# The ternary feed-forward of the last layer, taken from a stage of its own into the chain of attention units

## The chip, the cores and the metric

The kernel runs on one core of one Trainium2 chip. The metric is the device time of one execution in microseconds; lower is better. The profile names the engines of the core PE (matrix multiply), PEld (its weight loads), DVE (vector), ACT (scalar), POOL (GpSimd) and SP (which issues most transfers).

## The reference

A decoder of four layers works on an activation `x` of 4 batches × 256 tokens × 128 features, which is 8 tiles of 128 tokens, two to a batch. Each layer adds a self-attention, a cross-attention and a feed-forward to `x`. This case is about the last layer, whose feed-forward has ternary weights and activations rounded to 8 bits:

```python
x = x + _L3_attn_ref(_layernorm(x), ...)            # 16 heads of 8, low-rank, causal
x = x + _L3_xattn_ref(_layernorm(x), ctx_1024, ...) # 16 heads of 8, 512 keys
x = x + _L3_ffn_ref(_layernorm(x), L3_ffn_w1, L3_ffn_w2)

def _quant_act(x):                                  # per token
    scale = 127.0 / jnp.clip(jnp.max(jnp.abs(x), axis=-1, keepdims=True), EPS, None)
    xq = jnp.clip(jnp.round(x * scale), -128.0, 127.0) / scale
    return x + jax.lax.stop_gradient(xq - x)
def _bitlinear(x, w):
    return jnp.einsum('bsi,oi->bso', _quant_act(x), _quant_weight(w))
h = jax.nn.gelu(_bitlinear(x, w1), approximate=False)   # 128 -> 512
return _bitlinear(h, w2)                                # 512 -> 128
```

## The kernel before, in words

All of `x` stays on chip (`x[t]` is tile t). The stages follow one another: `layer_0`, `ffn0`, `layer_1`, `ffn1`, the linear and the latent attention of layer 2, `ffn2`, `layer_3`, `quantised_ffn`, and eight transfers that write `x` to `out`. Instructions are written in an order that the code sets, and each engine works through its own in that order.

`layer_3` builds eight `Unit`s: units 0 to 3 are the self-attentions of the four batches, units 4 to 7 their cross-attentions. `woven` runs them as one chain. It cuts each unit into steps, gives each step a time on a scale on which one unit takes 1.0, sorts by that time and emits. What falls behind a unit's own 1.0 is carried into the next unit. So in a stretch of the chain these stand side by side:

- the scores of the next unit by rows of queries (`rows_of`): PE writes `s`, and DVE reads it for the row's largest value `mx` (L477 to L481; with a mask, L481 goes over 128×512 values and a short read of the accumulator follows). In layer 3 two row tiles and two column tiles make a beat;
- the scores of this unit by columns of keys (`columns_of`): PE adds the mask (L522), less the maximum (L529) and the score (L535) into `s`, and ACT takes the exponential into `pr` (L552);
- the weighted sum of values (`weighted`, L571) into the only bank `o`, which ACT copies out at its end (`os`, L577); then division (L589, L591), transposing and `added` (L606 on PE, L610 on DVE), which adds the batch's result to `x`;
- the prelude of the unit after the next (`norm`, `source`, `queries`, `keys`), and `values`.

All tiles of `s` come from seven banks (`BANKS`: `"s1": 7`). A list `u.after` holds steps that are to follow a unit's `added`; the code spreads them over 2.6 units of time:

```python
late += spread(u.after, at + 2.1 * lag, at + 2.1 * lag + 2.6)
```

In this kernel only `layer_1` fills it (its strided cross-attention).

`quantised_ffn` comes after the chain has ended, has its own pools, and goes tile by tile: norm, `quantise` (largest absolute value `am`, L1950; scale `qs`, L1951 to L1954; its inverse `un`, L1956 and L1957; rounding and clipping `q`, L1959 and L1960), transposing through PE (`pt`, L311) with DVE as the reader (`qT`, L1964), the hidden matmul (`sc`, L1973), the exact Gelu on ACT (`h`, L1975), the same `quantise` on 512 values, four transposes, four matmuls (`ms`, L1979), and the sum into `x` (L1983). Only the Gelu needs another function table on ACT than the exponential of the chain. The ternary weights were made ready much earlier (`ternary_weights`).

Of the kernel before, what the change touches and what calls it, by code (L numbers as in the profile page):

```python
# [22 lines left out]
F32 = mybir.dt.float32  # L23
BF16 = mybir.dt.bfloat16
# [3 lines left out]
AF = mybir.ActivationFunctionType  # L28
ALU = mybir.AluOpType
AX = mybir.AxisListType  # L30
PSUM = bass.MemoryType.PSUM

P = 128
B, S, D, H = 4, 256, 128, 16
NT = B * S // P
# [5 lines left out]
EPS = 1e-5  # L41
# [3 lines left out]
MAGIC = 12582912.0  # L45
# [138 lines left out]
def decoder(ctx: ExitStack, tc: tile.TileContext, dr, out):  # L184
    nc = tc.nc
    V, A, G, T = nc.vector, nc.scalar, nc.gpsimd, nc.tensor

    const = ctx.enter_context(tc.tile_pool(name="const", bufs=1, reuse_waits="tile"))
    small = ctx.enter_context(tc.tile_pool(name="small", bufs=4, reuse_waits="tile"))
# [8 lines left out]
    def ps(tag):  # L198
        cols = 1024 if tag == "sc" else 512
        return psum[0].tile([P, cols], F32, tag=tag, name=tag, bufs=BANKS.get(tag, 2))  # L200

    @contextmanager
    def psum_pool(name):
        with tc.tile_pool(name=name, bufs=2, space=PSUM, reuse_waits="tile") as psum[0]:
            yield
# [14 lines left out]
    x = [xs[:, t, :] for t in range(NT)]  # L220
# [44 lines left out]
    turn = [0]  # L265
# [9 lines left out]
    def normalise(srcs, dsts, on=None):  # L275

        scaled_by(statistics(srcs), srcs, dsts, on)
# [20 lines left out]
    def scaled_by(stats, srcs, dsts, on=None):  # L298
        mv, rs = stats
        for i, (s, d) in enumerate(zip(srcs, dsts)):  # L300
            (on or V).tensor_scalar(
                d, s, mv[:, i, 0:1], rs[:, i : i + 1], ALU.subtract, ALU.mult
            )

    def transposed(srcs, dst, move=evacuate, tag="pt"):

        for c in range(0, len(srcs), 4):
            some = srcs[c : c + 4]
            tp = ps(tag)
            for i, s in enumerate(some):  # L310
                T.transpose(tp[:, i * P : (i + 1) * P], s, ident)  # L311
            move(dst[:, c * P : (c + len(some)) * P], tp[:, : len(some) * P])
# [26 lines left out]
    def product(lhsT, rhs, tag):  # L339

        n = int(np.prod(rhs.shape[1:]))
        acc = ps(tag)[:, :n]
        T.matmul(acc, lhsT=lhsT, rhs=rhs, start=True, stop=True)  # L343
        return acc
# [4 lines left out]
    def attn_pool(st, name):  # L349
        return st.enter_context(tc.tile_pool(name=name, bufs=2, reuse_waits="tile"))  # L350
# [18 lines left out]
    def spread(fns, start, end):  # L369

        n = len(fns)
        return [(start + (end - start) * (i + 0.5) / n, f) for i, f in enumerate(fns)]

    def call(f, *args):
        return lambda *more: f(*args, *more)

    class Unit:
# [7 lines left out]
        def __init__(u, b, nk, weights, prelude, context, q_bias=None, k_bias=None, v_bias=None,  # L385
                     rows_mask=None, row_mask=None, cols_mask=None, key_bias=None, clip=False):
            u.b, u.nk, u.weights, u.prelude, u.context = b, nk, weights, prelude, context
            u.q_bias, u.k_bias, u.v_bias = q_bias, k_bias, v_bias
            u.rows_mask, u.row_mask, u.cols_mask = rows_mask, row_mask, cols_mask
            u.key_bias, u.clip, u.nkt = key_bias, clip, nk // P  # L390
            u.mx, u.pr, u.po = None, {}, {}
            u.beside, u.after = [], []

    def woven(pool, units, n_keys):

# [3 lines left out]
        for i in range(2):  # L399
            t = pool.tile([P, n_keys // P, H, 32], F32, tag=f"v{i}", name=f"v{i}", bufs=1)  # L400
# [3 lines left out]
            t = pool.tile([P, 2, 4, 32], BF16, tag=f"mp{i}", name=f"mp{i}", bufs=1)  # L404
# [218 lines left out]
        def groups_of_columns(u):  # L623
            return [call(columns_of, u, gp, kt) for gp in (0, 2) for kt in range(u.nkt)]
# [12 lines left out]
        def halved(groups):  # L637
            return [(f, h) for f in groups for h in range(2)]
# [49 lines left out]
        def back(n):  # L688

            u = units[n]  # L690
            columns = groups_of_columns(u)
            out, most = beats(halved(columns), rows_in(n), units[n + 1] if n + 1 < len(units) else None)
            step = 1.0 / most

            lag = step if len(out) > 4 else 0.5 * step
            late = []
            for i in range(len(columns)):
                gp, kt = 2 * (i // u.nkt), i % u.nkt
                at = (i + 1) / len(columns) + 1.01 * step
                late += [(at, call(weighted, u, gp, kt, 0)), (at + lag, call(weighted, u, gp, kt, 1))]  # L700
                if kt == u.nkt - 1:
                    late += [(at + 2 * lag, call(divided_by_sums, u, gp))]
            at = late[-1][0]
            late += [(at + lag, call(transposed_result, u)), (at + 2 * lag, call(added, u))]
            late += spread(u.after, at + 2.1 * lag, at + 2.1 * lag + 2.6)
            return out, late

        def run(items):
# [14 lines left out]
        for n in range(len(units)):  # L723
            own, late = back(n)
# [1184 lines left out]
    wq3 = []  # L1909
# [26 lines left out]
            wq.append(qb)  # L1936
        return wq, ws

    def quantised_ffn():


        with ExitStack() as st:
            pool = st.enter_context(tc.tile_pool(name="l3f", bufs=3, reuse_waits="tile"))
            wq, ws = wq3

            def quantise(src, n, m):


                am = small.tile([P, 1], F32, tag="am", name="am")
                V.tensor_reduce(am, src, AX.X, ALU.max, apply_absolute_value=True)  # L1950
                V.tensor_scalar(am, am, EPS, None, ALU.max)  # L1951
                sc = small.tile([P, 1], F32, tag="qs", name="qs")
                V.reciprocal(sc, am)
                V.tensor_scalar(sc, sc, 127.0, None, ALU.mult)  # L1954
                un = small.tile([P, 1], F32, tag="un", name="un")
                V.reciprocal(un, sc)  # L1956
                V.tensor_tensor(un, un, ws[:, m : m + 1], ALU.mult)  # L1957
                q = pool.tile([P, n * P], F32, tag=f"q{n}", name=f"q{n}")
                V.tensor_scalar(q, src, sc, MAGIC, ALU.mult, ALU.add)  # L1959
                V.tensor_scalar(q, q, MAGIC + 127.0, MAGIC - 128.0, ALU.min, ALU.max)  # L1960
                qT = pool.tile([P, n * P], BF16, tag=f"qT{n}", name=f"qT{n}")
                transposed(
                    [q[:, i * P : (i + 1) * P] for i in range(n)], qT,
                    lambda d, s: V.tensor_scalar(d, s, MAGIC, None, ALU.subtract),  # L1964
                )
                return qT, un

            for t in range(NT):
                xn = pool.tile([P, D], F32, tag="xn", name="xn")
                normalise([x[t]], [xn])  # L1970
                qT, un = quantise(xn, 1, 0)
                hp = ps("sc")[:, :512]
                T.matmul(hp, lhsT=qT, rhs=wq[0], start=True, stop=True)  # L1973
                h = pool.tile([P, 512], F32, tag="h", name="h")
                A.activation(h, hp, AF.Gelu, scale=un)  # L1975
                qT, un = quantise(h, 4, 1)
                y = ps("ms")
                for ic in range(4):
                    T.matmul(  # L1979
                        y[:, :P], lhsT=qT[:, ic * P : (ic + 1) * P],  # L1980
                        rhs=wq[1][:, ic * P : (ic + 1) * P], start=ic == 0, stop=ic == 3,
                    )
                V.scalar_tensor_tensor(x[t], y[:, :P], un, x[t], ALU.mult, ALU.add)  # L1983


    def context_T(b):
# [69 lines left out]
    def layer_3():  # L2056
        with ExitStack() as st:
            st.enter_context(psum_pool("ps3"))
            pool = attn_pool(st, "l3")
            mc, mcT = (added_mask(pool, k, 2, True) for k in ("mcau", "mcauT"))  # L2060
            mf, mfT = added_mask(pool, "mif1", 2, False), added_mask(pool, "mif1T", NKT, False)
            units = low_rank_units(
                pool, w3a, rows_mask=lambda qt: mc[:, qt, :], cols_mask=lambda kt: mcT[:, kt, :]
            )
            units += cross_units(
                pool, w3x, 10, lambda b: None, rows_mask=lambda b: lambda qt: mf[:, qt, :],
                cols_mask=lambda b: lambda kt: mfT[:, kt, :],
            )
            woven(pool, units, SK)

    def other(*stages):
        with psum_pool(f"ps_{stages[0].__name__}"):
            for stage in stages:
                stage()

    with early:
        e0h = e0.tile([P, 32 * 512], F32, tag="e0h", name="e0h")
# [2 lines left out]
    late = ctx.enter_context(tc.tile_pool(name="late", bufs=1, reuse_waits="tile"))  # L2080
# [17 lines left out]
        latent_attention(held["w2kv"], held["w2qo"])  # L2098
    ffn2()
    layer_3()  # L2100
    other(quantised_ffn)
    for t in range(NT):
        nc.sync.dma_start(out[t * P : (t + 1) * P, :], x[t])


# [15 lines left out]
```

## Time and profile before

| | |
|---|---|
| median of 3 runs | 1584.9 us (1581.91 to 1585.73) |
| the profiled execution: its time, its span | 1585.49 us, 1583.7 us |
| busy over the span | PE 86%, PEld 44%, DVE 52%, ACT 46%, POOL 18% |
| mean granted clock of PE | 0.904 |
| `added` (L606) of the four cross-attentions starts at | 1419.8, 1461.0, 1502.1 and 1526.8 us |
| last `added` is complete (L610) | 1528.0 us |
| feed-forward of layer 3, first to last DVE result | 1528.0 to 1581.1 us |
| last write of `out` lands | 1583.7 us |

The span runs from the first instruction to the last; the execution's own time is 1.8 us more. A row of the profile tells the line in the code, the engine, what is written from what, how often, and the mean duration of one; "idle before, releaser" is how long the engine stood idle just before and whose result ended that. The table says that the feed-forward of the last layer takes 53 us alone at the end, two thirds of it with PE idle.

### The profile page before, as it was taken

To read this page: it belongs to the slowest core of one execution; us is meant where nothing else is said; L and a number is where in the kernel's file an instruction comes from. 1 tells how busy PE (TensorE), PEld (TensorE's weight loads), DVE (VectorE), ACT (ScalarE), POOL (GpSimd) and SP (SyncE) were. 2 spreads that over 40 slices of the span, in tenths; PEclk is the share of its full clock that TensorE was granted. 3 is DMA by queue.
4 is the path that set the end of the run, shared out by engine and by line. 5 is a ranking of instruction groups with operands and counts; after the bars stand their busy time and mean duration, and the time that the engine had idled before them with its cause. 6 is when DMAs were issued, how large, how long until landed. Compare 5 with 4: busy or idle time off the path is not lost.

```text
span 1583.7 us, 27050 instructions
## 1 busy us (share of the span) xinstructions
PE 1354.8 (86%) x10188; PEld 703.7 (44%) x10189; DVE 823.2 (52%) x2707; ACT 726.1 (46%) x1440; POOL 285.2 (18%) x417
## 2 busy tenths in 40 slices
PE   4997998787777998879999999999595699999963
PEld 2542333434345564544555555455363344333322
DVE  5676663484655346564444453351433566765336
ACT  0543566365642324367667656665021044344431
POOL 5223110164121415100000000000333521211000
PEclk8898999786987999999999999999697599999985
DMA  8000000321042215220111000000312000000000
GB/s 318 1 1 1 2 1 2 120 42 34 26 181 73 69 31 191 92 95 14 54 41 41 1 1 1 1 1 1 138 43 62 14 2 1 1 1 1 1 2 12
DMA packets 34980, 67.97 MB, mean 43 GB/s; under 512 B 5014, under 2 KB 18752, under 8 KB 32928
## 3 DMA queue, kind: packets, MB, share of 16 engines
q1 hardware_dynamic: 30434, 49.88, 8.9%
q0 software_dynamic: 3264, 6.69, 2.0%
q10 hardware_dynamic: 1152, 9.67, 1.5%
q8 instruction: 82, 1.34, 0.4%
q14 instruction: 48, 0.39, 0.1%
HBM read 49.55 MB, written 16.68 MB: 42 GB/s over the span
## 4 chain that ended last, share of the span: by engine, by line
PE 71%; DVE 12%; ACT 6%; issue 5%; POOL 4%; DMA 1%; ACTq 0%; DVEq 0%; POOLq 0%; SPq 0%
PE s L535 7%; PE o L571 7%; PE s L470 6%; PE o L1839 6%; PE g L1079 5%; PE s L1819 5%; PE f L1768 4%; PE s L522 3%; PE y L1103 2%; PE f L1754 2%; PE s L529 2%; PE f L1724 2%; PE s L343 2%; PE s L1812 2%; DVE mx L477 1%
## 5 line engine op out<-in xcount | busy, mean ns | idle before, releaser
L470 PE MATMUL s<-kc,qm 32*128 32x256 f32 (+1 forms) x1024 | 221.7, 569 | 13.9 <-POOL qm L425 8.3
L552 ACT ACTIVATE pr<-s 128x512 f32<-128x512 f32 x256 | 137.9, 596 | 195.9 <-PE s L535 185.7
L535 PE MATMUL s<-qm,kc 32*128 32x512 f32 (+1 forms) x896 | 211.7, 618 | 0.0
L477 DVE TENSOR_REDUCE mx<-s 128x1 f32<-128x512 f32 (+1 forms) x192 | 122.5, 685 | 70.3 <-PE s L535 54.5
L1779 ACT ACTIVATE ss<-ss,ntop 128x768 f32<-128x768 f32 x128 | 118.6, 928 | 85.6 <-DVE ntop L1777 85.3
L571 PE MATMUL o<-pr,v 128*32 128x256 f32 (+1 forms) x1792 | 146.8, 394 | 9.0 <-ACT os L577 4.1
L293 POOL TENSOR_SCALAR ve<-mv 128x2 f32<-128x2 f32 (+1 forms) x56 | 12.6, 226 | 774.3 <-DVE mv L288 709.8
L1773 DVE CUSTOM_DVE_ANT_0 ss<-f,n 128x512 f32<-128x512 f32 x128 | 83.4, 689 | 75.2 <-PE f L1768 75.2
L470 PEld LDWEIGHTS s<-kc,qm 32*128 32x128 f32 x1024 | 89.5, 207 | 70.1 <-issue 17.7
L481 DVE CUSTOM_DVE_ANT_0 junk<-s,nmif 128x512 bf16<-128x512 f32 x128 | 83.0, 688 | 54.0 <-PE s L470 53.7
L1839 PE MATMUL o<-pr,v 128*64 128x256 f32 x768 | 109.5, 397 | 0.0
L554 ACT ACTIVATE pr<-s,n 128x512 f32<-128x512 f32 x128 | 80.1, 690 | 62.5 <-PE s L535 43.4
L1819 PE MATMUL s<-qT,kT 64*128 64x256 f32 x768 | 103.1, 385 | 0.0
L571 PEld LDWEIGHTS o<-pr,v 128*32 128x32 f32 x1792 | 40.6, 110 | 118.9 <-issue 90.3
L1826 ACT ACTIVATE pr<-s,n 128x512 f32<-128x512 f32 x128 | 80.2, 678 | 20.9 <-PE s L1819 20.7
L529 PE MATMUL s<-mT,selg 12*128 12x256 bf16 x768 | 81.3, 280 | 9.2 <-DVE mx L477 5.9
L425 POOL TENSOR_SCALAR qm<-q,consts 128x256 f32<-128x256 f32 x64 | 58.5, 930 | 160.0 <-ACT q L422 129.5
L1057 POOL DMA_INDIRECT xb<-sent,token x62 | 60.3, 973 | 114.7 <-PE t L1064 58.3
L1761 DVE CUSTOM_DVE_ANT_0 ss<-f,nought 128x256 f32<-128x256 f32 x128 | 46.7, 421 | 60.8 <-PE f L1754 60.7
L1768 PE MATMUL f<-kT,qT 64*128 64x512 f32 x256 | 76.2, 624 | 0.1
L1839 PEld LDWEIGHTS o<-pr,v 128*64 128x64 f32 x768 | 48.1, 137 | 60.6 <-issue 23.8
L1819 PEld LDWEIGHTS s<-qT,kT 64*128 64x128 f32 x768 | 68.3, 192 | 6.2 <-issue 0.2
(407 smaller groups left out, 2415.8 us busy)
## 6 DMA issues: line engine op xcount, KB each, us to landing
e0h<-in_e0h SPq DMA_DIRECT2D x8, 1024.0 KB
kd<-ahead SPq DMA_DIRECT2D x20, 256.0 KB
vd<-ahead SPq DMA_DIRECT2D x20, 256.0 KB
kT<-kd SPq DMA_DIRECT2D x20, 256.0 KB
v<-vd SPq DMA_DIRECT2D x5, 1024.0 KB
e0d<-in_e0d SPq DMA_DIRECT2D x1, 4096.0 KB
e1h<-in_e1h ACTq DMA_DIRECT2D x1, 4096.0 KB
done<-ys SPq DMA_DIRECT2D x14, 256.0 KB
```

Of the source, the lines that this page charges most:

```text
L470: T.matmul(sc[:, i, :], lhsT=u.qm[r, g + i, qt * P : (qt + 1) * P], rhs=u.kc[r, :], start=u.row_mask is None, stop=True,)
L477: V.tensor_reduce(u.mx[:, qt, j, g : g + per], sc, AX.X, ALU.max)
L481: V.tensor_tensor_reduce(junk[:, : u.nk], sc[:, i, :], u.rows_mask(qt), 1.0, -3e38, ALU.add, ALU.max, accum_out=u.mx[:, qt, j, g + i : g + ...
L529: T.matmul(sc[:, i, :], lhsT=selg[r, gp + i, :], rhs=u.mT[r, :], start=u.cols_mask is None and i == 0, stop=False,)
L535: T.matmul(sc, lhsT=u.kc[r, kt * P : (kt + 1) * P], rhs=u.qm[r, gp : gp + 2, first:], start=u.clip, stop=True,)
L552: A.activation(dst, sc, AF.Exp)
L571: T.matmul(u.po[gp][32 * j : 32 * j + 32, i, first:], lhsT=u.v[:, kt, 4 * j + gp + i, :], rhs=u.pr[gp, kt, j][:, i, first:], start=kt + i ...
L1768: T.matmul(sc[h], lhsT=qT[u, c][hrow[h], qt * P : (qt + 1) * P], rhs=kT[u, c][hrow[h], :SK], start=True, stop=True,)
L1773: V.tensor_tensor_reduce(ss[qt][h][:, :SK], sc[h], neg1[:, b * SK : (b + 1) * SK], 1.0, -3e38, ALU.add, ALU.max, accum_out=mx[:, qt, h, 1:2],)
L1779: A.activation(ss[qt][h], ss[qt][h], AF.Exp, bias=ntop[:, qt, h, c : c + 1], accum_out=total[:, qt, h, c : c + 1],)
L1819: T.matmul(sc[h][:, i, :], lhsT=kT[u, c][hrow[h], kt * P : (kt + 1) * P], rhs=qT[u, c][hrow[h], :], start=False, stop=i == 1,)
L1839: T.matmul(po[u, g][hrow[h], i, :], lhsT=v[u][:, kt, n * hd : (n + 1) * hd], rhs=pr[u, g, kt, h][:, i, :], start=kt + i == 0, stop=kt + i ...
```

## The change

`quantised_ffn`, which worked on one tile at a time in a stage of its own, becomes `quantised_steps`, a list of eight steps for the two tiles of one batch: `norm`, `quantise`, `turn`, `hidden`, `quantise_hidden`, `turn_hidden` for each of the two tiles, `result`. The list of batch b is put into `u.after` of its cross-attention (units 4 to 7), with a new length `u.within` of 0.8 units in place of the 2.6. The steps take their `s` tiles from the chain's seven banks. The small statistics are made for two tiles in one instruction, the norm's last step goes to POOL, and the second transposed activation is read out by ACT (a Copy with a bias) where DVE did it before. The writes of `out` follow each batch's `result`.

```diff
-            u.beside, u.after = [], []
+            u.beside, u.after, u.within = [], [], 2.6
...
-            late += spread(u.after, at + 2.1 * lag, at + 2.1 * lag + 2.6)
+            late += spread(u.after, at + 2.1 * lag, at + 2.1 * lag + u.within)
...
+    def quantised_steps(pool, b):
+        wq, ws = wq3
+        u = {}
+        def quantised(src, m, tag):
+            am = small.tile([P, 2], F32, tag="am", name="am")
+            V.tensor_reduce(am, src, AX.X, ALU.max, apply_absolute_value=True)
+            V.tensor_scalar(am, am, EPS, None, ALU.max)
+            sc = small.tile([P, 2], F32, tag="qs", name="qs")
+            V.reciprocal(sc, am)
+            V.tensor_scalar(sc, sc, 127.0, None, ALU.mult)
+            un = small.tile([P, 2], F32, tag="un", name="un")
+            V.reciprocal(un, sc)
+            V.tensor_scalar(un, un, ws[:, m : m + 1], None, ALU.mult)
+            q = pool.tile(list(src.shape), F32, tag=tag, name=tag)
+            for i in range(2):
+                V.tensor_scalar(q[:, i], src[:, i], sc[:, i : i + 1], MAGIC, ALU.mult, ALU.add)
+            V.tensor_scalar(q, q, MAGIC + 127.0, MAGIC - 128.0, ALU.min, ALU.max)
+            return q, un
+        def norm():
+            two = [x[2 * b], x[2 * b + 1]]
+            u["xn"] = pool.tile([P, 2, D], F32, tag="xq", name="xq")
+            normalise(two, [u["xn"][:, i] for i in range(2)], G)
+        def quantise():
+            u["q"], u["un"] = quantised(u["xn"], 0, "q1")
+        def turn():
+            u["qT"] = pool.tile([P, S], BF16, tag="qT1", name="qT1")
+            transposed(
+                [u["q"][:, i] for i in range(2)], u["qT"],
+                lambda d, s: V.tensor_scalar(d, s, MAGIC, None, ALU.subtract), tag="s1",
+            )
+        def hidden():
+            hp = [product(u["qT"][:, i * P : (i + 1) * P], wq[0], "s1") for i in range(2)]
+            u["h"] = pool.tile([P, 2, 512], F32, tag="h", name="h")
+            for i in range(2):
+                A.activation(u["h"][:, i], hp[i], AF.Gelu, scale=u["un"][:, i : i + 1])
+        def quantise_hidden():
+            u["qh"], u["unh"] = quantised(u["h"], 1, "q4")
+            u["qhT"] = pool.tile([P, 2, 512], BF16, tag="qT4", name="qT4")
+        def turn_hidden(i):
+            transposed(
+                [u["qh"][:, i, c * P : (c + 1) * P] for c in range(4)], u["qhT"][:, i],
+                lambda d, s: A.activation(d, s, AF.Copy, bias=-MAGIC), tag="s1",
+            )
+        def result():
+            y = ps("s1")
+            for i in range(2):
+                for c in range(4):
+                    T.matmul(
+                        y[:, i * P : (i + 1) * P], lhsT=u["qhT"][:, i, c * P : (c + 1) * P],
+                        rhs=wq[1][:, c * P : (c + 1) * P], start=c == 0, stop=c == 3,
+                    )
+            for i in range(2):
+                t = 2 * b + i
+                V.scalar_tensor_tensor(
+                    x[t], y[:, i * P : (i + 1) * P], u["unh"][:, i : i + 1], x[t], ALU.mult, ALU.add
+                )
+                nc.sync.dma_start(out[t * P : (t + 1) * P, :], x[t])
+        return [
+            norm, quantise, turn, hidden, quantise_hidden, call(turn_hidden, 0),
+            call(turn_hidden, 1), result,
+        ]
...
+            for u in units[B:]:
+                u.after, u.within = quantised_steps(pool, u.b), 0.8
             woven(pool, units, SK)
...
     layer_3()
-    other(quantised_ffn)
-    for t in range(NT):
-        nc.sync.dma_start(out[t * P : (t + 1) * P, :], x[t])
```

## The prediction

> **What bounds the kernel now.** First the busy time by stretches, cut where each cross-attention's `added` starts and where the last one ends. Columns: length, then busy us (instructions) of PE, PEld, DVE, ACT, POOL, then clock and transfers.
>
> ```profile
> 1419.82:1460.97 41.15, 41.15 (x376) 14.51 (x372) 24.48 (x84) 19.40 (x37) 5.24 (x8) 1.00 0.01 1
> 1460.97:1502.06 41.09, 38.98 (x356) 13.95 (x353) 17.57 (x60) 18.27 (x35) 1.56 (x4) 1.00 0.00 1
> 1502.06:1528.00 25.94, 22.09 (x240) 9.11 (x236) 2.55 (x11) 13.83 (x27) 0.00 (x0) 1.00 0.01 1
> 1528.00:1583.70 55.70, 18.50 (x79) 10.99 (x80) 35.82 (x167) 6.78 (x9) 2.94 (x8) 0.52 0.03 10
> ```
>
> The chain of units is PE's; DVE is half free and ACT half. After it no engine is full. Second, the chain of waits there, one period of the tile loop:
>
> ```profile
> 1556.51 0.70 ACT h L1975
> 1557.23 0.88 DVE am L1950 x2
> 1558.75 0.39 DVE q L1959
> 1559.28 0.32 DVE q L1960
> 1559.75 1.10 PE pt L311 x4
> 1560.87 0.70 DVE qT L1964
> 1561.62 0.61 PE ms L1979 x4
> 1562.23 0.44 PE sc L1973
> ```
>
> Gelu follows Gelu after 6.18 us through ACT, DVE and PE by turns: a chain of latencies. Third, the order in time of one beat of the chain of units, which shows what slack it has for guests:
>
> ```profile
> 1426.66 0.69 DVE L481 CUSTOM_DVE_ANT_0 junk<-s,nmif 128x512 bf16<-128x512 f32 x1 [0.99 <-PE s L470]
> ...
> 1426.83 1.09 ACT L552 ACTIVATE pr<-s 128x512 f32<-128x512 f32 x2 [1.19 <-PE s L535]
> ...
> 1427.28 0.69 DVE L481 CUSTOM_DVE_ANT_0 junk<-s,nmif 128x512 bf16<-128x512 f32 x1
> 1427.80 0.19 PEld L470 LDWEIGHTS s<-kc,qm 32*128 32x128 f32 x2 [0.42 <-ACT pr L552]
> ```
>
> A beat lasts 2.30 us. DVE is idle 0.99 of them, but its second read ends at 1428.0 and PE wants that bank again in the next beat at about 1428.3: DVE's guests are free only in the gap between reads. Fourth, one wait that grows:
>
> ```profile
> 1514.30 0.62 ACT L577 COPY os<-o 128x512 f32<-128x512 f32 x1
> 1514.97 0.16 PEld L571 LDWEIGHTS o<-pr,v 128*32 128x32 f32 x8 [1.62 <-ACT os L577]
> ```
>
> There is one bank for `o`, so PE waits for ACT's copy.
>
> **What the Trainium skill says.** "ScalarE: Activation LUTs", section "What ACT_TABLE_LOAD costs", gives 1283 ns for a load and about 1380 ns more for a drain. The trace agrees with the load (1283 ns in all 17 of latent attention and feed-forward) and not with the drain: at 1013.62 a load starts, at 1014.92 the next function. I take 1.30 us. "PSUM — Partial Sum Buffer", section "Engine vs sequencer instructions", says that ACT, DVE and POOL take their queues strictly in order, so a guest that waits holds up the reads behind it. "VectorE: DVE Perf Modes", section "The perf-mode tier table", has tensor_reduce at its slowest mode always; here `am` takes 277 ns for 128 values and 687 for 512, so I estimate 1.24 us for 1024.
>
> **Part 1, removed: the stage.** 1528.0 to 1583.7, 55.7 us.
>
> **Part 2, the tail that stays.** Batch 3 has no attention after it, so its two tiles run alone, once. From the rows of the stage and of the norms (POOL: `ve` 0.23, `rs` 0.72 for two, `xn` 0.82 each): statistics 0.8 (1421.06 to 1421.87), POOL 2.8 with a handover, `am` to `q` for 2×128 values 2.0, two transposes and their read 1.3, hidden matmuls and two Gelus 1.9, second quantise 3.65 (`am` 1.24, four small ones 0.65 as from 1576.52 to 1577.17, `q` 2×0.47, clipping 0.72 by the slope from 204 ns at 128 to 426 at 512, handover 0.1), two times four transposes 2.2 and the last ACT copy 0.8, four matmuls and two sums 1.4. Sum 16.85. The table load waits only for `un` and hides behind the transposes. The last write lands 2.6 us after the last sum, as before. So 19.5 us in place of 55.7: **36.2 saved**. The other writes move beside the chain; nothing stands behind them on SP.
>
> **Part 3, what the chain must take in**, three batches. The order of the built programs is the same up to batch 0's steps, so nothing earlier moves; after that it shows where each step stands.
> PE's own work per batch: two transposes 0.37, two hidden matmuls 0.45, eight transposes 2×0.59 (L586), eight bf16 matmuls 0.7 (0.6 to 1.2: four cost 0.61 at the end, at low clock). 2.7, times three **8.1**. It is bare, since PE has no gap in the first stretch.
> Stalls, worked by laying the built order on the durations:
> - *Norm and first quantise, batches 0 and 1.* `am` waits on POOL's `xq`, which comes 2.8 us after the statistics; POOL itself is free. I count from the end of the beat ahead, time 0. The statistics are done at 2.6, `xq` at 5.4, `am` at 5.85. In batch 0 one read of the beat that ends at 2.9 stands ahead of `am`, the other behind it, and ends at 6.5; the small ones, `q` and clipping keep DVE till 8.3; the first read of the beat that ends at 5.2 ends at 9.0. PE's next beat wants the first late bank at 5.8 and has it at 6.5, and the second at 7.0 and has it at 9.0. It ends at 9.9 where 7.5 was due: 2.4 us. In batch 1 no read stands ahead of `am`; the same count gives 2.1 on one beat and 0.7 on the next: 2.8. The read of the two transposes (0.42) and the two sums (0.35 each) fall into DVE's 0.99 us gap and are taken at nothing; without that gap they cost 1.1 per batch.
> - *Gelu and second quantise, batches 0 and 1.* ACT does load, Gelu, Gelu, load: 1.3+0.69+0.69+1.3 = 4.0 us without an exponential. Time 0 is again the end of the beat ahead: its exponentials are done at 1.24, the Gelus at 3.9, the second load at 5.2, the next beat's exponentials at 6.3. `weighted`, which needs them, comes at 6.65 behind the hidden matmuls, the division's transposes and the keys' product: hidden, with 0.35 us to spare. DVE waits for the second Gelu till 3.95 and then works 3.6 us with one read in between, to 8.5; one row bank is free at 5.9 for 5.45, the next at 9.2 for 8.25: 1.5 for batch 0, 1.1 by the same count for batch 1, which has a wait for `pr` there already; 0.5 more where ACT's copy of `qT4` (0.65) stands ahead of `mT`.
> - *Batch 2*, in the last unit: DVE has no rows to read, but ACT's beat is four exponentials, 2.06 us. The Gelus stand ahead of the copy `os`, so the wait shown above grows by load and two Gelus: 2.8 less 0.45 covered by the hidden matmuls. `turn` waits for `q` some 0.65; the end of the unit waits for `qT4`. With PE's work 5.7, so 3.0 of stall.
>
> Sum: 2.7+3.9, 2.7+4.4, 5.7 = **19.4**. Bounds: 2 if the 6.0 us in which PE idles in stretches two and three take PE's work and no stall comes; 35 if POOL's wait and every DVE and ACT guest is paid in full.
>
> **The sum.** 36.2 − 19.4 = 16.8 off 1585.49, the profiled execution's own time: 1568.7. That execution lies 0.6 above the median, so **1568.2** there.
>
> **The rivals.**
> 1. *All of it hides* but PE's work. For it: DVE and ACT are half idle in the first two stretches. Against it: row banks with 0.3 us of slack, queues in order. 36.2 − 8.1 = 28.1 gained: 1557; with PE's idle time used, 1552.
> 2. *DVE becomes the bound.* Each of its guests is paid one for one in batches 0 and 1: work 6.6 and the wait for `xq` 2.8, with PE's 2.7 makes 12.1 each, and 5.7: 29.9. 1579. For it: the late bank. Against it: 0.99 us of gap in each beat, and eight steps over 33 us.
> 3. *Slower: PE, in order, waits for every step.* The steps of a batch form a chain of 16.85 us. If PE comes to each transpose or matmul before its input and stands, it pays the chain, not the work: 4×16.85+2.6 = 70 against 55.7, about 1599. For it: `turn` in batch 2 comes 0.65 too soon by my count. Against it: steps are 0.8×41.1/8 = 4.1 us apart in batches 0 and 1 and 2.6 in batch 2, about as long as most of them take. It decides from 12 us per batch on, since 36.2/3 is 12.1.
> 4. *The steps aren't moved beside the attention.* Then about 1585 less little. The built order puts batch 0's, 1's and 2's Gelus between exponentials, so this is all but excluded.
>
> **How the numbers follow.** Likeliest 0.72: 1568.2, itself 1561 to 1576. Rival 1 0.12, rival 2 0.10 (a tenth of it within 0.3%), rival 3 0.04, rival 4 0.02. About 0.3% (4.8 us) is what a measurement of this kernel can tell from no change. Faster 0.91, within 0.04, slower 0.05. The range 1556 to 1580 takes in the likeliest, rival 2 and the upper half of rival 1.
>
> **What would show it.** Each step has a mark in the profile of the changed kernel. The tail from the last `added` to the end is 19 to 20 us. The stretches between `added` grow from 41.15, 41.09 and 25.94 to about 47.8, 48.2 and 31.6. ACT shows seven table loads at 1283 ns in layer 3 (four for Gelu, three back to the exponential). PE's weight loads of `s` show waits of 1 to 3 us on DVE's `mx` after each norm, and the wait on `os` in the last unit is above 4 us. If the stretches grow by less than 3 us, rival 1 holds; by 12 or more, rival 2 or 3, told apart by whether PE waits on `mx` or on the feed-forward's own `q` and `qT`. A tail far from 19.5 means that Part 2 is mis-sized.

## The result, and the profile after

| | before | after |
|---|---|---|
| median, first comparison | 1583.7 us (1581.91 to 1585.73) | 1559.7 us (1556.62 to 1568.04) |
| median, second comparison | 1581.8 us (1579.92 to 1586.12) | 1562.3 us (1561.41 to 1565.55) |
| profiled execution: its time, its span | 1585.49, 1583.7 us | 1556.62, 1554.8 us |
| from the end of the first cross `added` to the end of the span | 162.64 us | 143.25 us |

The ratio is 0.9856 in the first comparison (95% interval 0.9813 to 0.9900) and 0.9876 in the second (0.9849 to 0.9903). The two profiled executions differ by 28.9 us, but only 19.4 of them lie where the change lies. The other 9.5 us were there before: the first cross `added` of layer 3 is complete at 1411.55 us instead of 1421.06. Experiment 1 is about these.

All stretches below are cut at the ends of the four cross `added` (L610 before, L611 after); in the kernel before they are 41.62, 40.55, 24.78 and, to the end, 55.69 us. First the busy time by stretches of the kernel after (length, then busy us of PE, PEld, DVE, ACT, POOL, then clock):

```profile
1411.55:1458.61 47.06, 45.89 (x400) 17.10 (x396) 30.77 (x105) 24.56 (x43) 6.16 (x8) 1.00 0.01 4
1458.61:1504.11 45.50, 42.21 (x374) 16.21 (x376) 21.84 (x77) 23.03 (x42) 2.52 (x4) 1.00 0.02 4
1504.11:1535.56 31.45, 26.38 (x248) 10.99 (x241) 8.77 (x33) 17.82 (x32) 2.53 (x4) 0.92 0.02 5
1535.56:1554.80 19.24, 4.74 (x20) 2.67 (x20) 7.13 (x26) 3.74 (x5) 2.53 (x4) 0.50 0.02 7
```

The chain pays 5.44, 4.95 and 6.67 us, 17.1 together; the end goes from 55.69 to 19.24. 36.45 less 17.06 is the 19.4. The clock of 0.92 in the third stretch is new. Next the chain of waits in the tail (start, us, what), which runs once where the chain of the stage before ran eight times:

```profile
1541.26 0.70 PE s L311 x2
...
1543.12 1.27 ACT h L1983 x2
1544.41 1.23 DVE am L1950
...
1547.38 0.70 DVE q L1961
1548.13 1.98 PE s L311 x8
1550.14 0.61 ACT qT L1992
...
1551.43 0.35 DVE x L2005
```

It is still a chain of latencies, but for two tiles at once. Last the order in time at the two places where the prediction had a stall. Batch 0's norm and first quantise:

```profile
1413.51 1.58 POOL L301 TENSOR_SCALAR xq<-x,mv,rs 128x128 f32<-128x128 f32 x2
1415.12 0.42 DVE L1950 TENSOR_REDUCE am<-xq 128x2 f32<-128x256 f32 x1 [1.88 <-POOL xq L301]
1415.46 0.68 DVE L482 CUSTOM_DVE_ANT_0 junk<-s,nmif 128x512 bf16<-128x512 f32 x1
...
1418.33 0.18 PEld L471 LDWEIGHTS s<-kc,qm 32*128 32x128 f32 x1 [1.32 <-DVE mx L482]
```

DVE stands 1.88 us for POOL's `xq`, with a row read behind it, and PE's loads then wait 1.32 us for the `mx` of a later read (1.91 us behind the same steps in the second stretch). In the first stretch of the kernel before no wait on `mx` is longer than 0.42 us. And the wait on `os` in the last unit:

```profile
1515.71 1.28 ACT L1983 ACT_TABLE_LOAD   x1
1517.00 1.27 ACT L1983 ACTIVATE h<-s,un 128x512 f32<-128x512 f32 x2
1518.16 0.59 ACT L578 COPY os<-o 128x512 f32<-128x512 f32 x1
1518.76 1.28 ACT L553 ACT_TABLE_LOAD   x1
1518.79 0.16 PEld L572 LDWEIGHTS o<-pr,v 128*32 128x32 f32 x8 [2.81 <-ACT os L578]
```

Before, this wait was 1.62 us; now it is 2.81.

### The profile page after: what moved, and what is told of

Read it like the earlier page. It is cut to its first block, busy times and chain, and to the rows that moved or that the text cites. A ratio compares the mean times of both kernels' runs of the same rounds, so it can differ in the third digit from the quotient of the medians.

```text
span 1554.8 us, 26964 instructions
## 1 busy us (share of the span) xinstructions
PE 1344.3 (86%) x10189; PEld 697.4 (45%) x10189; DVE 811.3 (52%) x2631; ACT 737.6 (47%) x1454; POOL 290.6 (19%) x417
## 4 chain that ended last, share of the span: by engine, by line
PE 70%; DVE 11%; ACT 6%; POOL 5%; issue 5%; DMA 2%; SPq 1%; ACTq 0%; POOLq 0%; DVEq 0%
PE o L572 7%; PE s L536 7%; PE s L471 6%; PE o L1840 6%; PE g L1080 5%; PE s L1820 5%; PE f L1769 4%; PE s L523 3%; PE y L1104 2%; PE f L1755 2%; PE s L530 2%; PE f L1725 2%; PE s L1813 2%; POOL back L1153 2%; PE s L343 2%
## 5 line engine op out<-in xcount | busy, mean ns | idle before, releaser
L553 ACT ACTIVATE pr<-s 128x512 f32<-128x512 f32 x256 | 138.1, 596 | 190.5 <-PE s L536 180.3
L293 POOL TENSOR_SCALAR ve<-mv 128x2 f32<-128x2 f32 x52 | 11.8, 227 | 777.7 <-DVE mv L288 777.4
```

Of the source, the lines that this page charges most:

```text
L553: A.activation(dst, sc, AF.Exp)
```

## The experiments

My theory: the move pays because a dependent chain is run once instead of eight times, and the guests cost the chain PE's own work and a few waits at places that can be named. The rivals: the guests cost DVE's whole work; the 9.5 us ahead belong to the change; and, from experiment 6 on, that the place in the chain brings little and the regrouping brings the gain. Edits are shown against the kernel after, except in 5 (the kernel before) and 11 (against 8); of the edits of 8 and 12 only a part is shown. A guest is a step of the feed-forward that stands in the chain. In the table the stretches are in us.

| kernel | 1st | 2nd | 3rd | end | sum | first `added` ends at |
|---|---|---|---|---|---|---|
| before; again (5) | 41.62; 41.63 | 40.55; 40.54 | 24.78; 24.77 | 55.69; 55.65 | 162.6 | 1421.1; 1420.8 |
| after; again (1) | 47.06; 47.07 | 45.50; 45.50 | 31.45; 31.46 | 19.24; 19.30 | 143.3 | 1411.6; 1417.9 |
| 2 `xq` on DVE | 46.15 | 44.45 | 29.36 | 18.17 | 138.1 | 1412.9 |
| 3 empty step | 48.30 | 47.17 | 30.93 | 19.32 | 145.7 | 1420.5 |
| 4 no table loads | 46.15 | 44.69 | 27.95 | 19.25 | 138.0 | 1415.1 |
| 6 own stage | 43.96 | 43.04 | 24.70 | 34.41 | 146.1 | 1415.4 |
| 7 Gelus behind `os` | 47.06 | 46.78 | 29.79 | 19.30 | 142.9 | 1414.1 |
| 8 half of batch 2 at the end | 46.14 | 44.46 | 25.54 | 17.42 | 133.6 | 1414.3 |
| 9 no second quantise | 46.13 | 44.57 | 29.36 | 15.03 | 135.1 | 1410.6 |
| 10 half the spacing | 50.22 | 47.77 | 32.86 | 19.37 | 150.2 | 1419.8 |
| 11 on top of 8 | 45.35 | 44.06 | 25.06 | 17.68 | 132.2 | 1419.4 |
| 12 PE's work alone | 43.81 | 41.63 | 25.89 | 19.39 | 130.7 | 1414.9 |

Each row is one profiled execution. Experiments 1 to 4, 6 to 8 and 11 also have medians of four executions: against the kernel before beside them these fall by 15.9 to 29.0 us, each within 2 us of what the sums of the table say. Differences of a microsecond or two rest on the stretches alone.

**1. The kernel after once more.**

> The changed kernel once more. The stretches of layer 3 should come out as before (47.1, 45.5 and 31.4 us between the ends of the four `added`, and 19.3 us after the last) within 0.3 us each. What it tests is the 9.5 us by which the changed kernel reached its first cross `added` of layer 3 early (1410.3 against 1419.8 us), though nothing ahead of it is changed. Theory 'state of the execution' (PE's granted clock in the first 100 us was 0.97 against 0.88): the start of this `added` will differ from execution to execution, anywhere from 1409 to 1421, and its difference goes with the clock of the first 100 us. Theory 'it belongs to the change' (for instance through where buffers lie): it will be at 1410 to 1411 in each kernel that has this layer 3.

The stretches came again within 0.06 us, and the first `added` ended at 1417.87. Over all changed kernels, which are alike up to layer 3's guests, that point lies anywhere from 1410.6 to 1420.5 (experiments 1 to 8, which ran on one chip and have the kernel before among them, lie from 1412.9 to 1420.8). So it is no property of the change: the early 9.5 us of the first pair of profiles are a difference between two executions, and in the second comparison the medians differ by 19.4 us, as the stretches do. The PE clock of the first 100 us does not decide it, as I had guessed: experiment 3 had 0.95 there and ended at 1420.5, experiment 4 had 0.88 and ended at 1415.1.

**5. The kernel before once more.**

> The kernel before once more, one profile. Layer 3 should be as it was: 41.6, 40.6 and 24.8 us between the ends of the four `added`, 55.7 after. What is open is when the first of them ends (1421.1 us in the first profile of this kernel). Theory 'state of the execution': anywhere from 1411 to 1421, as in the five profiles of kernels with the changed layer 3 (1411.6, 1417.9, 1412.9, 1420.5, 1415.1). Theory 'the change brings it forward': 1421 again, within 0.5.

1420.8 again, which both theories allow, so this profile alone speaks for neither side. The times without a profile do: the kernel before, in the comparisons of this study, took from 1575.46 to 1586.12 us, a spread as large as that of the first `added`. With layer 3 fixed at 162.6, 1575.5 means, as an estimate, a first `added` near 1411 (1575.5 less 1.8 around the span, less 162.6). What drives it stays open.

**2. `xq` on DVE.**

```diff
-            normalise(two, [u["xn"][:, i] for i in range(2)], G)
+            normalise(two, [u["xn"][:, i] for i in range(2)])
```

> The last step of the norm (`xq`) goes from POOL to DVE. Theory 'the wait for POOL stalls the chain': `am` stands 1 us earlier instead of waiting 1.9 us, so batches 0 and 1 each get about 1 us shorter (stretches of about 46.1 and 44.5 in place of 47.1 and 45.5) and the tail 0.9 shorter (18.4 in place of 19.3); some 3 us less than the changed kernel as a whole. Rival 'DVE is the bound there': `xq` on DVE adds its own work (two instructions of some 0.2 us) and the stretches stay or grow by 0.4. The third stretch, which has no row reads on DVE, changes by less than 0.5 in both.

0.91, 1.05 and 1.07 us less in the first, second and last stretch, as the wait for POOL would have it. In the first stretch the whole 0.9 is gained by the time of `turn`: its first transpose comes 9.93 us after the `added`, and 10.85 in the kernel after. The third stretch, which I expected to stay, lost 2.1. That is PE's clock, in steps of 1 us (the last column but two). First the kernel after, then experiment 2, each from 1.0 us after PE goes on behind `os`:

```profile
1519.80:1520.80 1.00, 1.00 (x4) 0.00 (x0) 0.93 (x6) 0.84 (x2) 0.00 (x0) 0.64 0.00 0
1520.80:1521.80 1.00, 1.00 (x6) 0.71 (x4) 0.96 (x3) 0.68 (x2) 0.00 (x0) 0.50 0.00 0
1521.80:1522.80 1.00, 1.00 (x10) 0.40 (x12) 0.78 (x4) 0.89 (x2) 0.00 (x0) 0.50 0.00 0
1522.80:1523.80 1.00, 1.00 (x13) 0.29 (x6) 0.00 (x0) 0.00 (x0) 0.00 (x0) 0.65 0.00 0
```

```profile
1519.16:1520.16 1.00, 1.00 (x6) 0.26 (x3) 0.93 (x6) 0.93 (x3) 0.00 (x0) 1.00 0.00 0
1520.16:1521.16 1.00, 1.00 (x16) 0.58 (x18) 0.96 (x3) 1.00 (x3) 0.00 (x0) 1.00 0.00 0
1521.16:1522.16 1.00, 1.00 (x13) 0.58 (x6) 0.68 (x4) 0.48 (x1) 0.00 (x0) 1.00 0.00 0
```

The waits ahead are the same to 0.01 us in both (2.81 on `os`), and in one execution the clock falls to half for 0.72 + 1 + 1 + 0.70 = 3.4 us (a dip) and in the other it does not. The Trainium skill, "TensorE: Matmul & The Clock Gate", section "What's actually happening", has two rates, half and full, set by PE's activity in windows of 3413 ns that run freely; the half rate, the 3.4 us and the dependence on the execution agree with that. Its table puts the fall after an idle window of about 3.4 us; here the trace differs, since the longest idle time of PE itself in the 10 us ahead of the dip is 1.98 us. A second dip takes the last 1.8 us of the third stretch. I therefore take 29.36 as the third stretch without dips: no profile of the kernel after itself lacks them, but experiment 9, which leaves `xq` on POOL and has no dip there, shows 29.36 too. By this the guests' price is 15.0 us, and 2.1 us of clock.

**3. An empty step between norm and quantise.**

```diff
-            norm, quantise, turn, hidden, quantise_hidden, call(turn_hidden, 0),
+            norm, lambda: None, quantise, turn, hidden, quantise_hidden, call(turn_hidden, 0),
```

> An empty step between norm and quantise, so that two row reads of DVE stand ahead of `am` while POOL still works on `xq`. Theory 'what stalls is the row reads queued behind the waiting `am`': batches 0 and 1 lose 2 to 2.5 us of stall each (stretches of about 44.8 and 43.2), the tail stays at 19.3; some 4 us less in all. Rival 'PE waits for another reason at that place, so that the wait only moves': stretches within 0.5 us of 47.1 and 45.5. A third outcome would be that the later steps, now 3.6 instead of 4.1 us apart, run into each other: then the waits on `qT4` and on `os` grow and the sum is the same or more.

It did not test what it was built for. In the trace `am` stands where it stood, with the same wait of 1.88 us for `xq`: by this trace, and by that of experiment 6, such a step of DVE is put as early as its inputs allow, and the list's time sets only where PE's steps go. What moved were `turn` and `hidden`, to 14.76 and 19.64 us after the `added`, while `quantise_hidden` kept closer: `am` of the hidden layer waits 2.5 us for the Gelu, and PE 1.6 for the `q` behind it. The first stretch grew by 1.24: the third outcome of the expectation, though the waits that grew are on the Gelu and `q` and not on `qT4` and `os`. (In the second and third, half of the clock is missing for 3.4 us each, so they tell nothing.)

**4. No table loads.**

```diff
-                A.activation(u["h"][:, i], hp[i], AF.Gelu, scale=u["un"][:, i : i + 1])
+                A.activation(u["h"][:, i], hp[i], AF.Exp, scale=u["un"][:, i : i + 1])
```

> The hidden layer's function is the exponential in place of the Gelu (the result is another one for that reason): ACT's seven table loads of layer 3 (7 x 1.28 us) go, everything else stays. Theory 'ACT has slack in batches 0 and 1, and the loads cost only where PE waits for the copy `os`': first two stretches within 0.7 us of 47.1 and 45.5, the third 1.2 to 2.5 us shorter (29 to 30.2), tail within 0.3 (its load was hidden); 1.3 to 3.5 us in all. Rival 'ACT's bursts hold up PE in each batch': all three stretches 2.0 to 2.6 us shorter, 6 to 8 in all.

0.91 and 0.81 less in the first two stretches: above my 0.7, far below the rival's 2 to 2.6. The third lost 3.5, of which 2.1 is the clock (29.36 to 27.95 is 1.41, for two loads of 1.28). The tail did not change: its load was hidden.

**9. No second quantise.**

```diff
-            u["qh"], u["unh"] = quantised(u["h"], 1, "q4")
+            u["qh"], u["unh"] = u["h"], u["un"]
```

> The second quantise is left out of all batches (the Gelu's result goes into the transposes as it is, so the result of the feed-forward is another one); 3.65 us of DVE per batch and DVE's wait for the Gelu go, all other steps stay where they are. From the changed kernel and the stage kernel, the steps behind the first quantise cost 3.1 us in batch 0 and 2.5 in batch 1. Theory of the prediction, 'DVE's second quantise holds the row reads': 1.5 and 1.1 us less (stretches of 45.6 and 44.4). Rival 'that work falls into DVE's free time; what is paid is PE's own work and some of the table loads': stretches within 0.4 of 47.06 and 45.50. The third stretch should lose about nothing but the dip in PE's clock (29.4 to 31.5), the tail 3.7 (15.6).

0.93 and 0.93 less: between the two theories. The place is the same as in experiment 4. The two PE lines are the hidden matmul and the first transpose of its result, in the kernel after and then here:

```profile
1428.22 0.39 PE L343 MATMUL s<-wq,qT 128*128 128x512 bf16 x1
1438.08 0.44 PE L311 MATMUL s<-consts,q 128*128 128x128 f32 x2
```

```profile
1427.27 0.39 PE L343 MATMUL s<-wq,qT 128*128 128x512 bf16 x1
1436.21 0.44 PE L311 MATMUL s<-consts,h 128*128 128x128 f32 x2
```

9.86 against 8.94 us; without the table loads it is also 8.94, and so it is in experiment 12, where loads, Gelus and quantise are all gone. In batch 1 the same distance is 10.37 us, 9.57 without the loads, 9.46 without the quantise and 9.44 without any of them. So taking away either 2.6 us of ACT or 3.65 us of DVE gains the 0.9 us that taking away both gains, or nearly: it is one stall at the end of a series (load, Gelus, quantise), not two, and shortening the series at either end removes it. In the third stretch the second quantise cost nothing (29.36 as in experiment 2).

**6. The same steps as a stage of their own.**

```diff
-            for u in units[B:]:
-                u.after, u.within = quantised_steps(pool, u.b), 0.8
             woven(pool, units, SK)
+            steps = [quantised_steps(pool, b) for b in range(B)]
+            for at in range(8 + 2 * (B - 1)):
+                for b in range(B):
+                    if 0 <= at - 2 * b < 8:
+                        steps[b][at - 2 * b]()
```

> The same eight steps of two tiles, but in a stage behind the chain, the four batches' lists laid over each other with a skew of two steps; nothing is put into the chain. It parts what the regrouping brings from what the place in the chain brings. The three stretches of the chain should be those of the kernel before (41.6, 40.6, 24.8) within 0.5: then the changed kernel's 17.1 us more are the price of its guests. The stage: DVE's own work for eight tiles is 4 x 7.5 = 30 us; with the start and the end of the lists I expect 38 to 44 us, that is 12 to 18 less than the stage before, and 2 to 8 us more than the changed kernel's 17.1 + 19.3 = 36.4. Rival 'the place in the chain brings nothing, two tiles per instruction bring it all': 36 us or less. Rival 'the steps still wait for each other': 50 us or more.

1563.8 us, and 1579.7 for the kernel before beside it (ratio 0.9903, 0.9876 to 0.9931). By the trace 16.5 of the 19.4 us come without putting a single PE step of the feed-forward into the chain, and the place of the other six steps in the chain brings 2.8 (146.1 against 143.3; 4.9 if the kernel after had no dips). The ratios don't tell these two kernels apart, since their intervals overlap. Both my figures were off, for one reason:

```profile
1414.97 0.42 DVE L611 TENSOR_TENSOR x<-x,s 128x256 f32<-128x256 f32 x1
1418.96 0.42 DVE L1950 TENSOR_REDUCE am<-xq 128x2 f32<-128x256 f32 x1 [1.88 <-POOL xq L301]
```

Norm and first quantise, which need only DVE and POOL, stand right behind their batch's `added` though the code lists them after the chain. So the stage is 34.4 and not 38 to 44, and the chain still pays 2.34, 2.50 and −0.08 us: a clean measure of what norm and first quantise cost there. The 16.5 us are therefore at least three things together, which no run parts: two tiles to an instruction, four batches laid over each other, and norm and first quantise beside the chain.

**12. PE's work alone.** Turn, hidden and both `turn_hidden` and `result` of batches 0 to 2 become transposes and matmuls on inputs that are ready:

```diff
...
+        if b < B - 1:
+            nothing = lambda: None
+            return [
+                nothing, nothing, call(unread, [x[2 * b], x[2 * b + 1]]), hidden_alone, nothing,
+                call(unread, [x[2 * b]] * 4), call(unread, [x[2 * b + 1]] * 4), result_alone,
+            ]
```

> In batches 0 to 2 the steps keep only PE's instructions (two transposes, two hidden matmuls, eight transposes, eight bf16 matmuls, at the same places in the chain, on inputs that are ready, their results read by nobody); norm, both quantises, Gelus, copies and sums are left out there, so the result lacks three batches' feed-forward. It measures by itself the term that the prediction took as 2.7 us of bare PE work per batch. Theory of the prediction: stretches of 44.3, 43.2 and 27.5 (41.6, 40.55 and 24.8 and 2.7 each). Rival, from the other runs: of the changed kernel's 5.4 and 4.95 us in batches 0 and 1, norm and first quantise are 2.3 and 2.5 and the second quantise 0.9 and 0.9, so that 2.2 and 1.5 are left: stretches of 43.8 and 42.05, since PE has 2.1 us of idle time in the second; in the third, where PE idles 3.9 of 24.8 us, at most 2 (26.8).

2.19, 1.08 and 1.11 us. In the first stretch PE is never idle and its work is bare; in the second and third half of it goes into the time in which PE waited before.

Set beside the kernel after, step by step from each `added` on, this run also parts the waits. In the kernel after, `turn` comes 2.34 and 2.51 us later in batches 0 and 1; between `hidden` and the eight transposes stand 0.92 and 0.93 more; and in batch 1 there are 0.49 more ahead of `result`, where ACT's copy of `qT4` (0.63 us) stands ahead of `mT`. PE's wait there, in the kernel after and then here:

```profile
1493.85 0.42 PE L530 MATMUL s<-mT,selg 12*128 12x256 bf16 x7 [0.70 <-ACT mT L273]
```

```profile
1489.99 0.42 PE L530 MATMUL s<-mT,selg 12*128 12x256 bf16 x8 [0.21 <-ACT mT L273]
```

In batch 2 the execution without dips (experiment 2) has 2.54 us more between `hidden` and the eight transposes, the place of the Gelus and `os`, and 0.93 more behind the start of `result`, where PE waits for `qT4`:

```profile
1526.89 0.23 PEld L1999 LDWEIGHTS <-qT 128*128 128x128 bf16 x4 [0.93 <-ACT qT L1992]
```

No other piece differs by more than 0.08 us.

**10. Half the spacing.**

```diff
-                u.after, u.within = quantised_steps(pool, u.b), 0.8
+                u.after, u.within = quantised_steps(pool, u.b), 0.4
```

> `within` 0.4 in place of 0.8, so that the steps of a batch stand about 2 us apart in the chain and not 4. Theory 'a step costs little because its input is ready when PE comes to it; the spacing pays for that': PE comes to the eight transposes 2 to 4 us before the second quantise has their input, and waits on `q`; the first two stretches grow by 2 to 5 us each (49 to 52 and 47.5 to 50.5), the third too, since there the steps are closer still; the tail stays at 19.3. Rival 'the price is the work of the engines, wherever the steps stand': stretches within 0.7.

The waits of PE's loads in the first stretch (total us, times, longest):

```profile
PEld s L311 <- DVE q L1961: 2.7, 1, 2.7
PEld s L311 <- ACT pr L553: 2.2, 1, 2.2
```

Both are new: PE comes to `turn` before the first `q`, and to the eight transposes before the second. The last wait is put down to `pr`, but the transpose itself starts with `q`:

```profile
1437.86 0.63 PE L311 MATMUL s<-consts,q 128*128 128x128 f32 x4 [1.37 <-DVE q L1961]
```

The growth is 3.16, 2.27 and 3.50 against the kernel after (its third stretch without dips), of which by the clock (PE's busy time by the share that is missing, an estimate: 46.55 × 0.03 and 26.08 × 0.08) 1.4 and 2.1 are dips. That leaves 1.8, 2.3 and 1.4, at or just under the 2 us that I expected at least, and well above the rival's 0.7: the spacing keeps the guests cheap. The dip of the first stretch begins where the first of these waits ends, so it may be a part of the price as well; that is not shown.

**7. Batch 2's Gelus behind the copy `os`.** `hidden` of batch 2 gets a time one beat later.

```diff
-            late += spread(u.after, at + 2.1 * lag, at + 2.1 * lag + u.within)
+            late += [
+                (t + u.shift.get(i, 0.0) * step, f)
+                for i, (t, f) in enumerate(spread(u.after, at + 2.1 * lag, at + 2.1 * lag + u.within))
+            ]
...
+                u.shift = {3: 1.0} if u.b == 2 else {}
```

> For batch 2 alone, `hidden` comes one beat later, so that its table load and Gelus stand behind the copy `os` on ACT and not ahead of it. Theory of the prediction, 'the wait is for `os`, which stands behind the Gelus': PE's wait of 2.8 us on `os` goes, and the third stretch gets 2.5 us shorter (29.0 in place of 31.45). Rival 'ACT itself is full there': from the exponentials at 1513.6 to those at 1522.7 ACT is never idle in the changed kernel, so the wait only moves on to the exponentials `pr` behind the second table load, and the third stretch changes by less than 0.7. By up to 1.6 us less in both if PE's clock, which fell to about half at 1519.9 to 1523.7, stays up because PE's gap is cut in two.

```profile
1520.02 0.16 PEld L573 LDWEIGHTS o<-pr,v 128*32 128x32 f32 x8 [1.62 <-ACT os L579]
1526.36 0.42 PEld L311 LDWEIGHTS s<-consts,q 128*128 128x128 f32 x4 [2.84 <-ACT pr L554]
1526.39 0.63 PE L311 MATMUL s<-consts,q 128*128 128x128 f32 x4 [2.39 <-DVE q L1965]
```

The wait on `os` is back at its 1.62 us, and a wait of 2.84 stands at the eight transposes, for the second quantise that now comes later. The third stretch is 29.79, and 29.36 without the edit when the clock does not dip (experiments 2 and 9): nothing gained. The wait only moves, as the rival said. (The second stretch has a dip of 3.4 us.)

**8 and 11. Two tries at a better kernel.** In 8, `xq` is on DVE, batch 2's second half goes behind the last `added` (its first steps stand in 0.3 units), batch 3's second quantise is cut by tiles, and the last tile's write is issued by ACT. Of the edit, the lists:

```diff
...
+            two, three = steps[2][3:], steps[3]
+            steps[2] = steps[2][:3]
+            steps[3] = [
+                two[0], three[0], three[1], three[2], two[1], three[3], two[2], two[3],
+                three[4], two[4], three[5], three[6], three[7],
+            ]
...
```

> A try at a better version. `xq` on DVE as in e2; batch 2's second half (hidden to result) goes behind the last `added` and is woven into batch 3's list, so that the chain's last unit has no table load and no second quantise; in batch 3 the second `am` and clipping are made tile by tile; the last tile's write is issued by ACT's queue beside SP's. Expected against e2 (46.15, 44.45, 29.36, 18.17): first two stretches the same within 0.3; third 26 to 26.5 (24.8 of the kernel before, and norm, quantise and turn of batch 2); tail 18.5 to 20.5, since batch 2's 3.6 us of second quantise fit into the 3 us in which DVE waits for batch 3's turn, hidden and Gelus. Sum from the first `added` 135 to 137.5, where the changed kernel has 143.3. Rival 'DVE is the limit in the tail and pays for batch 2 in full': tail 22 to 23, sum 139, nothing gained over e2.

1551.1 us beside 1579.7 (ratio 0.9825, 0.9803 to 0.9848), by its stretches ahead of both kernels. The sum of 133.6 is below my range: the end took 17.42, less than in experiment 2, with a second batch's half inside it. DVE is busy 11.27 of the 17.42 us there. What made the end shorter is not parted: besides the edit, PE's clock was full for 3.4 us of it, and in experiment 2 it was half from 1.6 us after the last `added` to the end.

> On top of e8, each quantise has three small operations in place of five (largest value times 1/127, its reciprocal as the scale, and the product with the weight scale). DVE's small operations stand 0.2 us apart, and two of them go from the path of each quantise. Expected against e8 (46.14, 44.46, 25.54, 17.42): tail 0.8 less (16.6), the first two stretches 0 to 0.5 less each, the third the same within 0.2. Sum about 132.4 against 133.6. Rival 'the tail is not bound by DVE's path': tail unchanged.

```diff
-            V.tensor_scalar(am, am, EPS, None, ALU.max)
+            V.tensor_scalar(am, am, EPS, 1.0 / 127.0, ALU.max, ALU.mult)
...
-            V.tensor_scalar(sc, sc, 127.0, None, ALU.mult)
...
-            V.reciprocal(un, sc)
-            V.tensor_scalar(un, un, ws[:, m : m + 1], None, ALU.mult)
+            V.tensor_scalar(un, am, ws[:, m : m + 1], None, ALU.mult)
```

1549.2 us beside 1578.2 (0.9799, 0.9772 to 0.9825); the intervals of 8 and 11 overlap. The stretches fell by 0.8, 0.4 and 0.5 (8 has a dip in the last 1.6 us of the third), but the tail did not. Batch 3's first clipping starts 0.38 us earlier after the last `added` than in 8, its last eight transposes only 0.19 us earlier: both its `q` now stand ahead of the clipping of the first tile. PE's clock then stays at half, where it became full in 8, and the last two sums start 0.27 us later. So the 0.8 us were not found, and with two clocks this pair doesn't settle how far DVE's path bounds the tail.

## Why the prediction was right or wrong

**The sign, the mechanism and the tail** were right. The tail was 19.24 for 19.5; the one chain of latencies, Gelu after `un`, the second quantise of 3.65, is there row by row (the `am` put at 1.24 took 1.22, the clipping put at 0.72 took 0.69). Seven table loads at 1.28 us were there, and so were the waits of PE's loads on `mx` behind the norms, put at 1 to 3 us: 1.32 and 1.91.

**The chain** was put at 19.4 and took 17.06, and 15.0 without the clock. Term by term:

| term | predicted | shown |
|---|---|---|
| norm, first quantise, batches 0 and 1 | 2.4, 2.8 | 2.34, 2.50 (6) |
| Gelus, second quantise, batches 0 and 1 | 1.5, 1.1 | 0.93, 0.93 (9) |
| `qT4` ahead of `mT`, batch 1 | 0.5 | 0.49 (12) |
| PE's own work | 2.7 each, "bare" | 2.19, 1.08, 1.11 (12) |
| batch 2 in all | 5.7 | 4.6, and 2.1 of clock |

The terms of batch 0 add up to 5.46 of 5.44 and those of batch 1 to 5.00 of 4.95, so there the account is closed. **The step that failed is "It is bare, since PE has no gap in the first stretch":** it was true of the first stretch and was then multiplied by three. The stretches shown in the prediction had 2.1 and 3.9 us of PE idle time in the second and third, and half of PE's work went there. Its sum was too large as well, 2.7 for 2.19, where it is bare. **The second mis-sized term is the Gelu's.** It held the loads to be "hidden, with 0.35 us to spare" and DVE's work to cost 1.5 and 1.1; the runs show one stall of 0.9, which goes if either is taken away. So the path through DVE was right and its size too large, and the loads were a part of that path, not free beside it.

**Batch 2** came near the right size in part by luck: 5.7 stood for 4.6, and 2.1 us of clock, which were in no part of the prediction, made 6.7 of it. The wait on `os` was to pass 4 us; it was 2.81, and experiment 7 shows that it is not by itself what costs: without it PE waits at the next place. Of the 4.6, PE's work is 1.1, the place of the Gelus and `os` 2.5 (1.4 of these are the loads, by experiment 4), and `result` waits 0.9 for `qT4`, as the prediction said without a figure. The 0.65 for `turn` was not there (0.07). The clock also brought the sum for the whole chain nearer to its 19.4.

**The time.** The forecast was 16.8 us less than its profiled execution; the traces show 19.4 for the same stretches, the second comparison 19.4, the first 24.0. Of the 8.5 us between the forecast and the first median, 2.6 are the terms above. The rest fits what experiments 1 and 5 show: the time up to layer 3 differs by some 10 us between executions, so medians of a few runs move by several us.

**The rivals.** All hidden but PE's work (8.1) and DVE in full (29.9) are both excluded by 17.1. (With PE's idle time used, the first comes to 1551 by its own terms and not to 1552.) The slower case, PE waiting for each step, has its mechanism shown in experiment 10, but at half the spacing the price is 20.4 us without dips (150.2 less 19.4 less 106.95, less 3.5), still below the 36 that it needs. What I had no rival for is that most of the gain needs no PE step of the feed-forward in the chain (experiment 6).

## What to carry to other kernels

When a change regroups a stage and moves it, price the two apart: here the regrouping, with norm and first quantise beside the chain, brought 16.5 us, and the place of the other steps in the chain 2.8. Price a guest's PE work by each stretch's own idle time, and a series of steps that wait for each other (load, function, reduction) as one stall and not as a sum; a wait in the trace is a place to look at, not yet a price, until an edit that removes it makes the stretch shorter. And compare two traces by stretches that begin after the last common instruction, because what lies ahead can differ by more than the effect.

## What the runs showed of the hardware that I had not expected

Stretches of layer 3 came again to 0.06 us in the two executions of each of two kernels, while the time up to layer 3 differed by 6.3 us between the two of the kernel after, and by 10 us over all executions, whose kernels are alike up to there (1410.6 to 1421.1 at the same instruction). And PE's clock can fall to 0.50 for 3.4 us within a chain that is 84% busy; the same wait of 2.81 us was followed by such a dip in three executions (after, 1 and 3) and by none in two (2 and 9). The dip in the second stretch of experiment 7 cost 1.28 us, and the two of the kernel after 2.1.
